# Layer 1's f and g on the two halves of TensorE's columns, with transfers to the quarters in place of copies

## The chip, the cores and the metric

The kernel runs on one core of one Trainium2 chip. The metric is the device time of that core in microseconds (us), the median of several executions. Below, TensorE is the matrix engine (PE in the profile, PEld for its weight loads), VectorE is DVE, ScalarE is ACT, GpSimd is POOL, and SyncE is SP, which issues all transfers (DMAs) of this kernel from one queue. Everything is in float32.

## What is computed

Eight images of 32x32 tokens (N = 1024) with C = 256 channels go through two attention layers. Layer 0 has four heads; layer 1 has one head whose f and g have only 32 channels.

```python
# layer 0: x (8, 32, 32, 256), W_qkv (256, 4*768), W_out (1024, 256)
xf = x.reshape(B, -1, C)
qkv = jnp.einsum('bnc,cd->bnd', xf, W_qkv).reshape(B, -1, h, 3 * C)
q, k, v = jnp.split(qkv, 3, axis=-1)
atten = jax.nn.softmax(jnp.einsum('bihd,bjhd->bijh', q, k) * scale, axis=2)
res = jnp.einsum('bijh,bjhd->bihd', atten, v).reshape(B, -1, h * C)
x = jnp.einsum('bnd,dc->bnc', res, W_out) + b_out + xf
# layer 1: Wf, Wg (256, 32), Wh (256, 256)
f = jnp.einsum('bhwc,ck->bhwk', x, Wf) + bf
g = jnp.einsum('bhwc,ck->bhwk', x, Wg) + bg
h = jnp.einsum('bhwc,cd->bhwd', x, Wh) + bh
s = jnp.einsum('bik,bjk->bij', g_flat, f_flat)
o = jnp.einsum('bij,bjd->bid', jax.nn.softmax(s, axis=-1), h_flat)
y = gamma * o + x
```

## The kernel before, in words

**Layer 0.** The weights of a head are folded first (`fold_weights`: query with key weights into wqk, value with output weights into wvo), so that a head needs one projection of x. The products of queries with keys, and of probabilities with values, are made by a scheme of seven products and sums of blocks (`seven`, line 235 for its matmuls, lines 252, 258 and 264 for what takes them out of the matmul banks). A head is worked off in two blocks of 512 query tokens.

**Layer 1.** The tokens after layer 0 are turned by transfers and VectorE (`turn_rows`) into x1T, channels on partitions. `Layer1.queries` projects x1T with `wfg_sb`, whose 128 columns hold Wf twice and Wg twice, 32 columns each: one matmul over 128 columns gives f on partitions 0 to 63 (twice) and g on partitions 64 to 127 (twice), for 512 tokens at a time (line 435, tile pm_fg). `store_fg` takes them out: ScalarE adds the bias on the 64 partitions where the result stands (line 661), and VectorE copies it to the other 64 partitions (line 662). In the end f and g stand four times each, on all four quarters of 32 partitions. `Layer1.scores` needs that: four matmuls with 32 rows of weights each, on the four quarters, make the scores of four times 128 keys (line 697, tile ps_l). `values` makes h (line 455), `Softmax` and `row_products` the rest (line 776).

**The order.** Each engine's order is the order in which the program issues its instructions. The main loop goes over `steps`: the heads of an image with two blocks each, and layer 1 of the image before put in after head 1 (after head 3 for the last but one image). Within a step, `put(tasks, *at)` gives each task a place on a scale from 0 to about 10, and the tasks are issued in order of place. In the step of head 1 (head 3), block 0, the turned tokens arrive; in the same head's block 1 the task list of `queries` stands at 1.4, 1.5 and 3.5: a start, the first 512 tokens, the second 512. The following step, block 0 of layer 1, begins with the scores. The last image has its own tail (`final`), which uses `queries` too.

Before the loop, x and the weights are loaded, the identity for transposes is built by VectorE, the first image is transposed by TensorE (line 339), and the weights of the four heads are folded, in part during the first step: `fold` is the list of the tasks for heads 1 to 3, five a head (three transposing, two multiplying, lines 291 and 307), and the first step places them among its scores.

**Buffers that matter here.** "m0" is one buffer, used by layer 0's sums of probabilities (`first` in `sums`, line 574, read again at line 579) and by layer 1's softmax. "psm" is a pair of matmul banks for everything but the scores and `seven`. "q" holds the queries of a head, or f and g of an image (`fg_tile`). "rs" is one small buffer for sums.

The functions that the diff touches:

Of the kernel before, what the change touches and what calls it, by code (L numbers as in the profile page):

```python
# [10 lines left out]
F32 = mybir.dt.float32  # L11
AF = mybir.ActivationFunctionType
# [4 lines left out]
P = 128  # L17
# [3 lines left out]
def kernel(  # L21
# [51 lines left out]
    nc = tc.nc  # L73
# [3 lines left out]
    CK = w_f.shape[1]  # L77
    CC = C // P
    NT = N // P
    NB = 512  # L80
    NBLK = N // NB
    HT = NB // P
# [10 lines left out]
    const = ctx.enter_context(tc.tile_pool(name="const", bufs=1))  # L93
# [15 lines left out]
    def tile_of(tag, shape, name):  # L109
        return pools[tag].tile(shape, F32, tag=tag, name=name)  # L110
# [4 lines left out]
    def load_x(b, parts=1):  # L115
        t = tile_of("rows", [P, NT, C], f"x_{b}")
        n = HT // parts
        for k in range(NBLK):
            for i in range(parts):
                nc.sync.dma_start(  # L120
                    t[:, k * HT + i * n : k * HT + (i + 1) * n, :].rearrange("p t c -> p (t c)"),
                    x_v[b][:, k, ts(i, n * C)],
                )
        rows[b] = t

    def identity():

        Q = 32
        t = const.tile([P, P], F32, tag="ident", name="ident")
        col = const.tile([P, Q], F32, tag="col", name="col")  # L130
        row = const.tile([P, Q], F32, tag="row", name="row")
        nc.vector.memset(col[:, 0:1], 0.0)
        w = 1
        while w < Q:
            nc.vector.tensor_scalar(col[:, w : 2 * w], col[:, :w], float(w), None, ALU.add)
            w *= 2
        nc.vector.transpose(row, col)
        nc.vector.memset(t, 0.0)
        for k in range(P // Q):
            r = ts(k, Q)  # L140
            nc.vector.tensor_tensor(t[r, r], col[r], row[r], ALU.is_equal)
        return t
# [4 lines left out]
    wfg_sb = const.tile([P, CC, P], F32, tag="wfg", name="wfg_sb")  # L147
    bout_sb = const.tile([P, C], F32, tag="bout", name="bout_sb")
    bfg_sb = const.tile([P, 1], F32, tag="bfg", name="bfg_sb")
    bh_sb = const.tile([P, C], F32, tag="bh", name="bh_sb")  # L150
    gamma_sb = const.tile([P, 1], F32, tag="gamma", name="gamma_sb")

# [2 lines left out]
    def load_rest():  # L155
        with nc.allow_non_contiguous_dma(reason="small bias vectors, loaded once"):
            nc.sync.dma_start(bout_sb, b_out.partition_broadcast(P))
            for r in range(P // CK):
                w, bias = (w_f, b_f) if r < P // CK // 2 else (w_g, b_g)
                nc.sync.dma_start(  # L160
                    wfg_sb[:, :, ts(r, CK)], w.rearrange("(cc p) k -> p cc k", p=P)
                )
                nc.sync.dma_start(bfg_sb[ts(r, CK), :], bias.unsqueeze(1))
            nc.sync.dma_start(wh_sb, w_h.rearrange("(cc p) d -> p cc d", p=P))
            nc.sync.dma_start(bh_sb, b_h.partition_broadcast(P))
            nc.sync.dma_start(gamma_sb, gamma.partition_broadcast(P))
# [12 lines left out]
    def load_weights(h, tag):  # L179

        nw = CC * 3 * C
        t = tile_of(tag, [P, nw + CC * C], f"w_{h}")
        w = t[:, :nw].rearrange("p (c d) -> p c d", c=CC)
        wo = t[:, nw:].rearrange("p (c d) -> p c d", c=CC)
        nc.sync.dma_start(w, wqkv_v[:, :, ts(h, 3 * C)])
        nc.sync.dma_start(wo, wout_v[:, ts(h, CC), :])
        weights[h] = w, wo
# [141 lines left out]
    xT_of, x1T_of, xblocks, vblocks = {}, {}, {}, {}  # L329
# [136 lines left out]
    def values_tile(name):  # L466
        v = tile_of("v", [P, NT, CV], name)
        nc.gpsimd.memset(v[:, :, C : C + 1], 1.0)
        return v
# [174 lines left out]
    class Layer1:  # L644
# [19 lines left out]
        def queries(self):  # L664
# [7 lines left out]
                f"fg_{b}", lambda: wfg_sb, P, lambda: x1T_of[b], self.store_fg  # L672
            )

        def values(self):
            def start():
                self.v = values_tile(f"v_{self.name}")

            return [start] + project_rows(
                f"v_{self.name}", lambda: wh_sb, lambda: x1T_of[self.b],  # L680
                lambda t2, pm: nc.vector.scalar_tensor_tensor(
                    self.v[:, 2 * t2 : 2 * t2 + 2, :C], pm, gamma_sb,
                    bh_sb.unsqueeze(1).broadcast_to([P, 2, C]), ALU.mult, ALU.add,
                ),
            )
# [127 lines left out]
        engines={mybir.EngineType.PE, mybir.EngineType.DVE, mybir.EngineType.Activation}  # L813
    ))
    load_x(0, 2)
    ident = identity()
    load_weights(0, "s")
    load_weights(1, "rows")
    load_weights(2, "v")
# [20 lines left out]
    fold = fold_weights(1) + fold_weights(2) + fold_weights(3)  # L840
# [6 lines left out]
    def step(k):  # L847
        return steps[k] if 0 <= k < len(steps) else None
# [4 lines left out]
    for i, (a, blk) in enumerate(steps):  # L853
        l0 = isinstance(a, Layer0)
        one, two, nxt = step(i - 1), step(i - 2), step(i + 1)
        places = []

        def put(tasks, *at):
            assert len(tasks) == len(at)
            places.extend(zip(at, range(len(places), len(places) + len(at)), tasks))  # L860

        if l0:
            put(a.scores(blk), 0, 2, 4, 6, 8, 10)
        else:
            tasks, pieces = a.scores(blk)
            put(tasks, *((0.5, 2.4) if blk == 0 else (0.5, 2)))
            put(pieces, *((1.6, 3.9, 6.2, 6.5, 7.4, 8.4, 8.6) if blk == 0 else
                          (0.9, 2.7, 4.2, 5, 6.2, 6.8, 7.5)))
        if is_l0(two):
            u, k = two  # L870
            put(u.products_of[k][2:], 1 if l0 else 0)
            put([partial(u.invert, k)], 2.9 if l0 or blk == 1 else 1.9)
            put(u.project(k), *((3, 7) if l0 else (2, 6) if blk == 0 else (3, 7)))
        if is_l0(one):
            u, k = one
            sums, keys = u.sums(k)
            u.products_of[k] = u.products(k)
            put(sums[:2] + sums[3:], *((2.2, 3.2, 4.2) if l0 else (0.8, 2.2, 4.5)))
            put(sums[2:3], 5.2 if l0 else 5.5)
            put(keys, *((6.2, 8.2) if l0 else (7.6, 9.6)))  # L880
            put(u.products_of[k][:2], *((5, 9) if l0 else (4, 7)))
        elif one is not None:
            put(one[0].products(one[1]), *((3, 5, 7, 9) if l0 else (1, 4, 6, 8)))
        if i == 0:
            put(fold[2:], -1, *[0.9 + 0.6 * n for n in range(len(fold) - 3)])
            put(first_sums[:2], 8.4, 9.4)
        if i == 1:
            put(first_sums[2:], 1.4, 3.4)
            put([partial(nc.vector.tensor_scalar, bh_sb, bh_sb, gamma_sb, None, ALU.mult)], 8.5)

        if is_l0(nxt) and blk == NBLK - 1:
            queries, qsums = nxt[0].queries()
            put(queries, *((2.5, 4.5, 6.5) if not l0 else
                            (1.5, 2.5, 4.5) if is_l0(two) else (0.5, 2.5, 5.5)))
            put(qsums, *((6.7, 6.9, 7.3, 7.6) if not l0 else
                          (5.4, 6.4, 7.2, 7.4) if is_l0(two) else (6.4, 7.2, 7.3, 7.4)))

        if l0 and a.h == 0 and blk == 0:
            put(residual(a.b), 5.3, 6.3, 7.3, 7.4)
        if l0 and a.h == 0 and blk == 1 and a.b > 0:  # L900
            put(value_sums(a.b), 1.4, 2.4, 3.4, 4.4)
        if l0 and a.h == 2 and blk == 0 and a.b + 1 < B:
            load_x(a.b + 1)
        if l0 and a.h == 2 and blk == 1 and a.b + 1 < B:
            moves, squares = turn_rows(a.b + 1, rows, xT_of, 0)
            put(moves, *range(1, 9))
        if l0 and a.h == HEADS - 1 and blk == 0 and a.b + 1 < B:
            put(squares, 0.4, 1.4, 2.4, 4.4)
            put(key_sums(a.b + 1), 5.4, 6.4, 7.2, 7.4)

        if l0 and a.b > 0 and a.h == behind(a.b) - 1:
            if blk == 0:
                moves, turned = turn_rows(a.b - 1, rows1, x1T_of, 1, step(i + 2)[0].fg_tile)
                put(moves, 0.1, 0.2, 0.3, 0.4)
                put(turned, 5.4, 6.4, 7.2, 7.4)
            else:
                put(nxt[0].queries(), 1.4, 1.5, 3.5)
        if not l0 and blk == 0:
            put(a.values(), 0.9, 1, 3, 5, 8)
        if nxt is None:  # L920
            put(transpose_rows(B - 1, rows1, x1T_of, 1), 8.1, 8.2, 8.3, 8.4)
            put(final.queries(), 9, 9.1, 9.3)
        for _, _, t in sorted(places, key=lambda x: x[:2]):
            t()
# [136 lines left out]
```

## Time and profile before

Three executions took 2358.72, 2360.36 and 2360.5 us; the profiled one took 2358.68 us, with a span of 2356.9 us in the profile and a mean granted TensorE clock of 0.999.

| group of instructions | what it is | count | busy us | mean ns |
|---|---|---|---|---|
| line 235, psy, TensorE | one of the score products of layer 0 | 1024 | 262.9 | 379 |
| line 626, po, TensorE | output projection of layer 0 | 1024 | 242.0 | 379 |
| line 776, pa_l, TensorE | layer 1, probabilities by values | 1024 | 231.7 | 381 |
| line 697, ps_l, TensorE | layer 1, scores on row quarters | 256 | 36.5 | 640 |
| line 366, fg<-x, SP | transfers that turn layer 1's tokens, 64 KB each | 112 | - | 2.3 us to landing |
| lines 586 and 589, SP | a row of sums turned into columns | 64 each | - | 2.1 us to landing (589) |

Busy time is what the records cover; matmul records overlap their neighbours, so the mean of one is longer than the time from one start to the next. In a group's line of the profile, what follows the second bar is the idle time of that engine just before these instructions, and what ended it.

### The profile page before, as it was taken

The numbers are of one execution on the slowest core, as the hardware profiler recorded it, in microseconds if no ns is written. First come the engines' busy times: TensorE is split into PE (matmuls) and PEld (weight loads), VectorE is DVE, ScalarE is ACT, GpSimd is POOL, SyncE is SP. The second block draws the span as 40 slices with busy tenths as digits, with TensorE's granted clock in tenths as the row PEclk, the third lists the DMA queues.
The fourth block names the chain that finished last, engine by engine and source line by source line (L and its number), as shares of the span: only waits on it lengthen the run. The fifth ranks groups of instructions, "written<-read, shape, count | busy, mean of one in ns | idle before, by whom it ended". The sixth has DMA issues, their size and how long they took to land.

```text
span 2356.9 us, 26075 instructions
## 1 busy us (share of the span) xinstructions
PE 2336.5 (99%) x10384; PEld 1923.2 (82%) x10384; DVE 1617.1 (69%) x2533; ACT 590.7 (25%) x945; POOL 236.6 (10%) x93
## 2 busy tenths in 40 slices
PE   8999999999999999999999999999999999999998
PEld 6888888788877888788887888878888788888877
DVE  5667777577775767767777577676776757766665
ACT  2222223222232222322223222232222322212232
POOL 0111110011110111101111011110001101100110
PEclk9999999999999999999999999999999999999999
DMA  4000010100101001010010000110001100000100
GB/s 136 1 1 1 1 36 4 34 1 9 28 5 32 1 19 19 8 29 1 19 19 13 24 1 19 19 17 20 1 19 19 19 18 1 1 1 1 19 10 29
DMA packets 163602, 38.35 MB, mean 16 GB/s; under 512 B 156112, under 2 KB 158160, under 8 KB 163472
## 3 DMA queue, kind: packets, MB, share of 16 engines
q1 hardware_dynamic: 163472, 36.60, 7.6%
q8 instruction: 84, 1.38, 0.2%
q14 instruction: 46, 0.38, 0.1%
HBM read 13.37 MB, written 8.52 MB: 9 GB/s over the span
## 4 chain that ended last, share of the span: by engine, by line
PE 95%; DVE 4%; DMA 0%; ACT 0%; issue 0%; SPq 0%; DVEq 0%; ACTq 0%
PE psy L235 14%; PE psy_y L235 14%; PE pa_l L776 9%; PE psx L235 9%; PE psz L235 9%; PE po L626 9%; PE psx_y L235 9%; PE psz_y L235 9%; PE psy_q L235 4%; PE psx_q L235 2%; PE psz_q L235 2%; PE pr_v_l L455 2%; PE pm_fg L435 1%; PE ps_l L697 1%; DVE s_l L758 1%; DVE s L569 0%
## 5 line engine op out<-in xcount | busy, mean ns | idle before, releaser
L582 POOL PARTITION_ALL_REDUCE rb<-rs x64 | 207.0, 3234 | 1891.5 <-DVE rs L580 1891.5
L530 ACT ACTIVATE p<-p 128x1024 f32<-128x1024 f32 x128 | 135.3, 1057 | 536.8 <-DVE p L252 536.8
L235 PE MATMUL psy<-qs,xs 128*128 128x256 f32 x1024 | 262.9, 379 | 1.7 <-DVE qs L501 1.7
L235 PE MATMUL psx<-q,x0T 128*128 128x256 f32 x1024 | 262.8, 379 | 0.0
L235 PE MATMUL psz<-q,xs 128*128 128x256 f32 x1024 | 262.8, 379 | 0.0
L235 PE MATMUL psy_y<-s,xt 128*128 128x256 f32 x1024 | 243.0, 380 | 2.5 <-DVE s L569 2.4
L626 PE MATMUL po<-wvo,y 128*128 128x256 f32 x1024 | 242.0, 379 | 0.0
L235 PE MATMUL psx_y<-p,x 128*128 128x256 f32 x1024 | 241.9, 379 | 0.0
L776 PE MATMUL pa_l<-v_l,s_l 128*128 128x257 f32 x1024 | 231.7, 381 | 2.3 <-DVE y L252 1.9
L235 PEld LDWEIGHTS psx<-q,x0T 128*128 128x128 f32 x1024 | 194.4, 190 | 43.0 <-issue 18.2
L626 PEld LDWEIGHTS po<-wvo,y 128*128 128x128 f32 x1024 | 194.5, 190 | 40.0 <-issue 15.1
L776 PEld LDWEIGHTS pa_l<-v_l,s_l 128*128 128x128 f32 x1024 | 193.7, 190 | 39.0 <-issue 12.6
L235 PEld LDWEIGHTS psx_y<-p,x 128*128 128x128 f32 x1024 | 194.6, 190 | 34.1 <-issue 8.6
L235 PEld LDWEIGHTS psy_y<-s,xt 128*128 128x128 f32 x1024 | 192.2, 190 | 34.7 <-PE psx_y L235 5.0
L235 PEld LDWEIGHTS psy<-qs,xs 128*128 128x128 f32 x1024 | 194.5, 190 | 28.5 <-DVE qs L501 2.1
L235 PEld LDWEIGHTS psz<-q,xs 128*128 128x128 f32 x1024 | 194.6, 190 | 26.5
L252 DVE TENSOR_TENSOR u<-psy,e 128x512 f32<-128x512 f32 x128 | 88.5, 691 | 148.1 <-PE psy L235 74.7
L264 ACT ACTIVATE p<-psx 128x512 f32<-128x512 f32 x128 | 76.4, 597 | 409.7 <-PE psx L235 409.5
L252 DVE TENSOR_TENSOR v<-psy,e 128x512 f32<-128x512 f32 x128 | 87.9, 687 | 101.8 <-PE psy L235 101.6
L235 PE MATMUL psy<-qs,x0T 128*128 128x256 f32 x512 | 131.5, 379 | 0.8 <-DVE v L252 0.8
L258 ACT COPY e<-psx 128x512 f32<-128x512 f32 x128 | 73.9, 577 | 202.3 <-PE psx L235 202.3
L637 DVE SCALAR_TENSOR_TENSOR x<-po,inverse,x 128x256 f32<-128x256 f32 x256 | 111.9, 478 | 17.6 <-PE po L626 7.3
(110 smaller groups left out, 3091.1 us busy)
## 6 DMA issues: line engine op xcount, KB each, us to landing
out_dram<-x SPq DMA_DIRECT2D x15, 512.0 KB, 2.6
x<-in_x_dram SPq DMA_DIRECT2D x14, 512.0 KB, 4.6
x0T<-x SPq DMA_DIRECT2D x224, 32.0 KB, 2.0
fg<-x SPq DMA_DIRECT2D x112, 64.0 KB, 2.3
w<-in_L_conv_W_qkv_dram SPq DMA_DIRECT2D x4, 768.0 KB
x<-in_x_dram SPq DMA_DIRECT2D x4, 256.0 KB, 4.5
w<-in_L_conv_W_out_dram SPq DMA_DIRECT2D x4, 256.0 KB, 9.5
line<-rb SPq DMA_DIRECT2D x64, 2.0 KB
```

The lines of the kernel that those rows point to most:

```text
L235: nc.tensor.matmul(banks[k][:, ts(i, w)], lhsT=lhsT, rhs=rhs, start=first and n == 0, stop=True, skip_group_check=True,)
L252: nc.vector.tensor_tensor(dst, shaped(banks[k]), shaped(other), ALU.add)
L258: nc.scalar.copy(scratch("e"), banks["x"])
L264: copy(outs["11"](), shaped(banks["x"]))
L435: nc.tensor.matmul(pm[:m], lhsT=w()[:, c, d * P : d * P + m], rhs=src()[:, c, ts(k, NB)], start=(c == 0), stop=(c == CC - 1),)
L455: nc.tensor.matmul(pm[:, ts(j, C)], lhsT=src()[:, c, ts(2 * t2 + j, P)], rhs=w()[:, c, :], start=(c == 0), stop=(c == CC - 1),)
L530: exp(both, both)
L582: nc.gpsimd.partition_all_reduce(t, r.rearrange("p e i -> p (e i)"), P, bass_isa.ReduceOp.add)
L626: nc.tensor.matmul(pm[:, ts(j, C)], lhsT=self.y[blk][:, c, ts(2 * t2 + j, P)], rhs=folded[self.h][1][:, c, :], start=(c == 0), stop=(c == ...
L637: nc.vector.scalar_tensor_tensor(acc, pm[:, ts(j, C)], inverse[:, n : n + 1], acc, ALU.mult, ALU.add)
L697: nc.tensor.matmul(pm, lhsT=self.f[ts(r, CK), ts(j0 + r, P)], rhs=self.g[ts(r, CK), ts(blk, NB)], start=True, stop=True,)
L776: nc.tensor.matmul(pm[:, : C + 1], lhsT=p[:, j, ts(ti, P)], rhs=v[:, j, : C + 1], start=(j == 0), stop=(j == NT - 1),)
```

## The change

There are three parts.

1. For images 0 to 6, `queries_apart` takes the place of `queries` in the loop. It uses only 64 of the columns of `wfg_sb`, those that hold Wf once and Wg once. The first 512 tokens go to columns 0 to 63 and so to partitions 0 to 63 of one bank, the second 512 tokens to columns 64 to 127 and partitions 64 to 127 of another bank; the four matmuls are issued in turn (first half, second half, then the same for the other 128 channels). Two activations on ScalarE add the bias (a second bias tile, `bfg2_sb`, has it in the order f, g, f, g) and put the result into a tile in the buffer m0. From there 16 transfers an image bring f and g to the four quarters, f only those 128-token pieces that a quarter's matmuls read, g whole. The copies on VectorE are gone. All matmuls stand at place 1.5, the transfers at 1.6 to 1.9.
2. Before the first transposes, VectorE clears a tile (`idle`) and TensorE multiplies it with itself five times; nothing reads the result.
3. In the first step, the task `multiply` wqk of head 1 moves from place 0.9 to ahead of the scores.

```diff
+    bfg2_sb = const.tile([P, 1], F32, tag="bfg2", name="bfg2_sb")
...
+                nc.sync.dma_start(bfg2_sb[ts(r, CK), :], (b_f, b_g)[r % 2].unsqueeze(1))
...
+        def queries_apart(self):
+            b = self.b
+            half, quarters = P // 2, P // CK
+            made = {}
+
+            def task():
+                fg = self.fg_tile()
+                self.f, self.g = fg[:, 0, :], fg[:, 1, :]
+                made["t"] = t = tile_of("m0", [P, NB], f"fg2_{b}")
+                w = wfg_sb[:, :, half - CK : half + CK]
+                pms = [tile_of("psm", [P, NB], f"pm_fg{k}_{b}") for k in range(NBLK)]
+                for c in range(CC):
+                    for k, pm in enumerate(pms):
+                        nc.tensor.matmul(
+                            pm[ts(k, half)],
+                            lhsT=w[:, c, :],
+                            rhs=x1T_of[b][:, c, ts(k, NB)],
+                            start=(c == 0),
+                            stop=(c == CC - 1),
+                        )
+                for k, pm in enumerate(pms):
+                    r = ts(k, half)
+                    nc.scalar.activation(t[r], pm[r], AF.Identity, bias=bfg2_sb[r])
+
+            def move(r):
+                q = ts(r, CK)
+                for k in range(NBLK):
+                    f, g = (made["t"][k * half + i * CK : k * half + (i + 1) * CK] for i in range(2))
+                    nc.sync.dma_start(self.f[q, ts(k * HT + r, P)], f[:, ts(r, P)])
+                    nc.sync.dma_start(self.g[q, ts(k, NB)], g)
+
+            return [task], [partial(move, r) for r in range(quarters)]
...
+    idle = tile_of("rs", [P, P], "idle")
+    nc.vector.memset(idle, 0.0)
     ident = identity()
+    pm = tile_of("psm", [P, NB], "pm_idle")
+    for _ in range(5):
+        nc.tensor.matmul(pm[:, :P], lhsT=idle, rhs=idle, start=True, stop=True)
...
         if i == 0:
-            put(fold[2:], -1, *[0.9 + 0.6 * n for n in range(len(fold) - 3)])
+            put(fold[2:], -2, -1, *[1.5 + 0.6 * n for n in range(len(fold) - 4)])
...
             else:
-                put(nxt[0].queries(), 1.4, 1.5, 3.5)
+                tasks, moves = nxt[0].queries_apart()
+                put(tasks, 1.5)
+                put(moves, 1.6, 1.7, 1.8, 1.9)
```

## The prediction

> **What bounds the kernel now.** I read the page from its first part down: busy time, the chain that ended last, the groups of the stage that changes; then the timeline of one image's stage, the DMA queue around it, and the start.
>
> ```profile
> PE 2336.5 (99%) x10384; PEld 1923.2 (82%) x10384; DVE 1617.1 (69%) x2533; ACT 590.7 (25%) x945; POOL 236.6 (10%) x93
> PE 95%; DVE 4%; DMA 0%; ACT 0%; issue 0%; SPq 0%; DVEq 0%; ACTq 0%
> L435 PE MATMUL pm_fg<-x1T,wfg_sb 128*128 128x512 f32 x64 | 30.0, 594 | 0.2 <-ACT x1T L342 0.2
> L661 ACT ACTIVATE fg<-pm_fg,bfg_sb 64x512 f32<-64x512 f32 x32 | 21.8, 683 | 65.4 <-PE pm_fg L435 65.0
> L662 DVE COPY fg<-fg 64x512 f32<-64x512 f32 x32 | 13.5, 422 | 22.1 <-ACT fg L661 21.7
> ```
>
> TensorE is idle for 20 of 2357 us and carries 95% of the chain: a stretch is worth what it takes or gives TensorE. The copies at L662 wait for L661, and hardly anything on TensorE waits for either. "x64" is 8 images by 4 matmuls by 2 records: an f32 matmul leaves two. Matmuls overlap, so I take the distance from start to start. The stage of image 0 in the timeline (start, duration, engine, operation):
>
> ```profile
> 358.19 1.88 PE L435 MATMUL pm_fg<-x1T,wfg_sb 128*128 128x512 f32 x4
> 359.91 1.03 PE L235 MATMUL psx<-q,x0T 128*128 128x256 f32 x4
> 363.36 1.88 PE L435 MATMUL pm_fg<-x1T,wfg_sb 128*128 128x512 f32 x4
> 365.08 1.03 PE L235 MATMUL psy<-qs,x0T 128*128 128x256 f32 x4
> 384.94 1.89 PE L235 MATMUL psz_y<-ss,x 128*128 128x256 f32 x8
> 386.76 1.14 PE L697 MATMUL ps_l<-fg 32*128 32x512 f32 x8
> 387.83 1.99 PE L455 MATMUL pr_v_l<-wh_sb,x1T 128*128 128x256 f32 x8
> 389.66 1.89 PE L626 MATMUL po<-wvo,y 128*128 128x256 f32 x8
> ```
>
> Four records of 512 columns take 359.91-358.19 = 1.72 us, 0.43 each; eight of 256 columns also take 1.72. So f and g of an image cost 2 x 1.72 = 3.44 us of TensorE. The lower half shows what parts of the array can do: the scores put four matmuls on four groups of 32 rows, and their eight records take 1.07 us to the next start, where one after the other they would take 3.44.
>
> **What the Trainium skill says.** "TensorEngine Tiling (Array Packing)", section Key Properties: tiles work independently, and a change of tiling mode drains TensorE. Both show above. "TensorE: Matmul & The Clock Gate", section Measured speedup vs the span model: three column tiles gave 2.38 times, four row tiles 3.07; the row group here gives 3.44/1.07 = 3.2, and no run here shows columns. Same page, Part 1: TensorE starts at half clock until about 3.4 us of activity. The first transposes do run slowly, but that is over when the weights land (below).
>
> **The change part by part.**
>
> *f and g on column halves, images 0 to 6.* Eight records of 64 columns of weights replace eight of 128; pairs that stand on different halves can run together, so four rounds of 0.43 = 1.72 us are the floor. To that comes the tiling. From the row group: the stage before it should give way at 384.94+1.72 = 386.66, the group starts 0.10 later; inside, two rounds take 1.07 for 0.86, 0.21 too many; the stage after it takes 1.83 for 1.72, 0.11 too many. Entry and exit are paid once (0.21); the 0.21 inside belongs to the group or to each two rounds. That bounds an image at 2.14 and 2.35; I take 2.25. Gain 3.44-2.25 = 1.19, times 7 = **8.3 us** (7.6 to 9.1). Row groups are not column groups, which no record shows: the ends beyond this are the rivals below.
>
> *Removed copies and half of the evictions.* 7x4 copies x 0.422 = 11.8 us of VectorE, 7x2 activations x 0.683 = 9.6 us of ScalarE. Price 0: both lie beside TensorE's 99%. They offset that TensorE comes earlier: v follows psy's start by 1.06 us (as at 378.23 below), so it would run at 362.36 instead of 361.99, and s, which TensorE's psy_y needs, would be done at 367.1, where TensorE arrives at 367.3. Bound 0.1 us an image.
>
> *Sixteen transfers an image (eight of 32x128, eight of 32x512), 112 in all, on SP's queue.* VectorE and SP in the same stretch:
>
> ```profile
> 354.45 0.38 SPq L589 DMA_DIRECT2D st<-line  x1
> 384.12 0.23 SPq L586 DMA_DIRECT2D line<-rb  x1
> 374.59 1.22 DVE L574 TENSOR_TENSOR m<-ss 128x1024 f32<-128x1024 f32 x1
> 376.51 0.88 DVE L637 SCALAR_TENSOR_TENSOR x<-po,inverse,x 128x256 f32<-128x256 f32 x2 [0.70 <-PE po L626]
> 378.23 0.69 DVE L252 TENSOR_TENSOR v<-psy,e 128x512 f32<-128x512 f32 x1 [0.85 <-PE psy L235]
> 381.48 1.03 PE L235 MATMUL psy<-qs,x0T 128*128 128x256 f32 x4
> 329.48 8.04 SPq L366 DMA_DIRECT2D fg<-x  x12
> ```
>
> ScalarE would finish at about 362. SP issued twelve fg<-x transfers in 8.04 us, 0.67 each, and those land after a median 2.3 us; so 16 x 0.67 = 10.7 and 2.3 later, by 375.0, all are there. The small st took SP 0.38, which would make it 370.4. SP is otherwise free from 355 to 384, so neither the line and st behind them nor POOL waits. TensorE's scores want f and g at about 385.5: hidden. The new wait is VectorE's m (L574): its buffer m0 is where the transfers read, so it now waits for all sixteen. Without one it would start at 374.59-1.19 = 373.4. Behind it in VectorE's order are x<-po and v, and TensorE's third psy (381.48, then 380.3) waits for v. From m to the end of v is 1.22+0.88+0.69 = 2.8, so m may start at 377.4 before TensorE loses anything. The landing at 370.4 to 375.0 costs 0 to 1.6 us of VectorE's idle time and nothing of TensorE's. Price 0. The semaphore waits in front of the scores lie on TensorE's queue and are satisfied by then; 0 (up to 0.1 an image). Both matmul buffers psm are taken at once; the next po needs one, freed by the first activation at 361.2, before po at 362.2; 0.
>
> *The start.* The multiply of weights 1 is moved ahead of the first scores:
>
> ```profile
> 21.75 1.03 PE L235 MATMUL psx<-q,x0T 128*128 128x256 f32 x4
> 24.51 1.13 PE L235 MATMUL psy<-qs,xs 128*128 128x256 f32 x4 [1.73 <-DVE qs L501]
> 26.34 1.89 PE L307 MATMUL pwqk<-wqT 128*128 128x256 f32 x8
> ```
>
> TensorE waits 1.73 us for VectorE's qs. pwqk (1.72) needs copies that end by 20.8 and now fits from 21.75 to 23.47; psx follows, psy keeps 24.51, and what came after pwqk comes 1.72 earlier. VectorE's u moves behind wqk and its sums, to 28.3; the second psy wants it at 28.8. **1.7 us** (0 to 1.8: a later wait could take it back, and nothing there makes it lose).
>
> *Zeros first.* Ten records and a memset of about 0.17 us while x is on its way; the first transpose waits for x until 4.0. The chain of waits goes through the arrival of the first weights at 8.76, and TensorE is at full clock from then on already (pwq's four records of 128 columns take 0.63 us, px's fourteen before took 3.34). 0 (to +1 in an execution where the clock rises later). Four more bias loads on SP delay wh, bh, gamma and the second x by some us; none is wanted before 60 us. 0.
>
> Sum: 8.3+1.7 = 10.0 us, against the profiled span of 2356.9: 2346.9. That execution took 2358.68 us; the others shown 2358.72 to 2360.5, median 2360.36. 2360.4-10.0 = **2350.4**.
>
> **The rivals.**
> 1. *Halves overlap only in part.* Each matmul's two records stand one after the other on the same half. If TensorE keeps that order, record 2 runs beside record 3 only, giving five rounds, 2.15+0.42 = 2.57: gain 0.87 x 7 + 1.7 = 7.8, at 2352.6. Against it: the row group, written in the same order, ran its four first records together.
> 2. *No overlap: the change doesn't do what it says.* Columns share the rows through which data and weights come; row groups do not, so their evidence need not carry over. Then 8 x 0.43 + 0.42 = 3.86, with 0.21 for each two rounds 4.5: 0.4 to 1.06 lost an image, 2.9 to 7.4 in all, less 1.7: 2361.6 to 2366.1.
> 3. *Slower: the wait at m0.* Place: VectorE's m at L574. If the sixteen land after 377.4, TensorE's psy waits as much longer; from 378.6 the gain on columns is gone, and from 379.5 (gain of the start used up, and 4.7 us more, over 7) the kernel is measurably slower. That needs 0.95 us a transfer. For it: while the weights load, SP's small wfg and bfg transfers come 2.73 us a pair, 1.37 each (issues at 11.48, 12.22, 14.21, 14.94, 16.94 and 17.68), since each waits for an earlier one. At 1.37, landing is at 362+21.9+2.3 = 386.2, 8.8 us late: 7 x (8.8-1.2)-1.7, so 2412. Against it: then the queues were full, here they are empty, and 0.67 was kept up through twelve transfers of more pieces.
>
> **How the numbers follow.** Full overlap 0.65 (gain 7.6 to 10.9: 2349.5 to 2352.8), part 0.13, none 0.13, m0 0.06, others 0.03. A measurement of this kernel can tell 0.2%, 4.7 us, from no change: the first two cases are faster than 2355.6; no overlap lies half within the bound and half above; m0 is slower. Faster 0.79, same 0.10, slower 0.11. The range: the bottom is an overlap without seams (7 x 1.72 + 1.8 = 13.8, 2346.6), the top takes in partial overlap with the gain of the start lost and some wait at m0: 2346.5 to 2358.5.
>
> **What would show it.** Right: 56 records of 64 columns whose image takes 2.1 to 2.4 us from first start to the next stage, in pairs some ns apart; psy at the start with no 1.7 us wait; m0's readers landed before 376. Wrong: the records 0.43 apart throughout (rival 2); a wait of VectorE at L574 for a DMA over 3 us, with a hole of TensorE before psy (rival 3); or a hole elsewhere in the stage as long as the gain.

## The result, and the profile after

The changed kernel takes 2347.29 us (median of 6 executions, 2346.37 to 2348.55), the kernel before, on the same chip, 2359.74 us (6 executions, 2357.71 to 2361.49): a ratio of 0.9948, with a 95% interval of 0.9935 to 0.9961. That is 12.4 us faster, in the range, and 3.1 us better than the 2350.4 forecast. The profiled execution took 2347.16 us with a span of 2345.4 us, against 2356.9 us before. In all comparisons of this document every execution lies within 0.2% of its kernel's median, but for one of the run e3 below, which took 6413.33 us and is not counted in its ratio.

The page of the kernel after, its busy times and its chain. Lines have moved: the scheme of seven products is at L237 now, the new matmuls are L693, their activations L702, the transfers L708 (f) and L709 (g), the last image's own L437, L663 and L664.

```profile
PE 2329.4 (99%) x10394; PEld 1917.0 (82%) x10394; DVE 1606.1 (68%) x2506; ACT 580.0 (25%) x931; POOL 236.5 (10%) x93
PE 95%; DVE 4%; DMA 0%; ACT 0%; issue 0%; SPq 0%; DVEq 0%; ACTq 0%
fg<-fg SPq DMA_DIRECT2D x56, 64.0 KB, 2.0
```

TensorE still carries 95% of the chain, so what is gained must be TensorE's. VectorE has 27 instructions fewer (28 copies removed, one memset added) and ScalarE 14. The groups of the stage:

```profile
L693 PE MATMUL pm_fg<-x1T,wfg_sb 128*64 128x512 f32 x56 | 13.6, 605 | 0.0
L702 ACT ACTIVATE fg<-pm_fg,bfg_sb 64x512 f32<-64x512 f32 x14 | 9.5, 682 | 42.1 <-PE pm_fg L693 42.0
L437 PE MATMUL pm_fg<-x1T,wfg_sb 128*128 128x512 f32 x8 | 3.7, 605 | 0.2 <-ACT x1T L344 0.2
L664 DVE COPY fg<-fg 64x512 f32<-64x512 f32 x4 | 1.7, 422 | 5.6 <-ACT fg L663 5.6
```

The records have a mean of 605 ns, about as long as before (594), but 56 of them cover 13.6 us, 1.94 an image, where 56 of the old ones stood 0.43 us apart and so took 24. The eight of the last image are of the old kind. The stage of image 0 in the timeline after (start, duration, engine, operation); the weight loads (PEld) show the order inside the group:

```profile
355.06 1.89 PE L237 MATMUL psz_y<-ss,x 128*128 128x256 f32 x8
356.88 0.20 PEld L693 LDWEIGHTS pm_fg<-x1T,wfg_sb 128*64 128x64 f32 x4 [0.33 <-issue]
356.88 1.94 PE L693 MATMUL pm_fg<-x1T,wfg_sb 128*64 128x512 f32 x8
357.36 0.14 PEld L693 LDWEIGHTS pm_fg<-x1T,wfg_sb 128*64 128x64 f32 x2 [0.29 <-issue]
357.79 0.14 PEld L693 LDWEIGHTS pm_fg<-x1T,wfg_sb 128*64 128x64 f32 x2 [0.29 <-issue]
358.75 1.13 PE L237 MATMUL psx<-q,x0T 128*128 128x256 f32 x4
```

Loads come in twos, 0.43 apart. Single records of the trace show the same of the matmuls: they start at 0 and 7 ns, 480 and 487, 910 and 916, 1339 and 1345 (image 3), and psx 1.87 us after the first. The two records that signal a finished half to ScalarE are both in the last pair, so a pair has one record of each half.

What the group costs beyond its four rounds of 0.43, I call its seams. psz_y should give way at 355.06+1.72 = 356.78, so the entry costs 0.10. Inside, the first round takes 0.48, 0.05 too many, and psx starts 0.53 after the last pair, 0.10 too many. At the exit, psx takes 0.10 more than its undisturbed 0.86. An image costs 1.87+0.20 = 2.07 us, that is 1.72 and 0.35 of seams, the same in all seven.

The transfers and what could wait for them, same timeline:

```profile
358.85 1.39 ACT L702 ACTIVATE fg<-pm_fg,bfg_sb 64x512 f32<-64x512 f32 x2 [6.00 <-PE pm_fg L693]
359.56 0.57 SPq L708 DMA_DIRECT2D fg<-fg  x1
...
369.54 0.59 SPq L709 DMA_DIRECT2D fg<-fg  x1
...
371.21 0.69 DVE L254 TENSOR_TENSOR u<-psy,e 128x512 f32<-128x512 f32 x1 [1.62 <-PE psy L237]
371.95 1.23 DVE L576 TENSOR_TENSOR m<-ss 128x1024 f32<-128x1024 f32 x1
373.73 0.88 DVE L639 SCALAR_TENSOR_TENSOR x<-po,inverse,x 128x256 f32<-128x256 f32 x2 [0.56 <-PE po L628]
375.45 0.69 DVE L254 TENSOR_TENSOR v<-psy,e 128x512 f32<-128x512 f32 x1 [0.85 <-PE psy L237]
378.71 1.03 PE L237 MATMUL psy<-qs,x0T 128*128 128x256 f32 x4
383.98 1.14 PE L735 MATMUL ps_l<-fg 32*128 32x512 f32 x8
```

The sixteenth transfer is issued at 369.54 and, by the median of 2.0, lands near 371.6. VectorE's m follows u at once, with no wait in brackets; psy and the scores have none either. (Over the seven images m waits for these transfers for 0.2 us at most, in image 6, and no wait of TensorE follows.) The start, where the fold moved:

```profile
9.20 0.63 PE L293 MATMUL pwq<-ident,w 128*128 128x128 f32 x4 [1.07 <-DMA w<-in_L_conv_W_qkv_dram]
...
22.06 1.89 PE L309 MATMUL pwqk<-wqT 128*128 128x256 f32 x8
23.79 1.03 PE L237 MATMUL psx<-q,x0T 128*128 128x256 f32 x4
24.82 1.13 PE L237 MATMUL psy<-qs,xs 128*128 128x256 f32 x4
```

The wait of 1.73 us in front of psy is gone; pwqk fills it. The weights landed 0.3 us later than in the profiled execution before (pwq at 9.20, then 8.90).

Where the time went: I compared the start of each TensorE record with its counterpart before. They are 0.31 later at 9 us, 1.41 earlier once the fold is done (so 1.72 gained), and then 2.78, 4.14, 5.49, 6.85, 8.20, 9.57 and 10.92 earlier after images 0 to 6. Nothing else on TensorE steps: seven times 1.36, and one 1.72. That makes 11.2 us. (The two profiled spans differ by 11.5: 0.3 was lost as the weights landed later, and 0.6 lies behind TensorE's last record: 6.1 us before, 5.4 to 5.9 in all the other traces.) The fastest executions of the two kernels lie 2357.71-2346.37 = 11.3 apart, so the remaining 1.2 of the 12.4 between the medians is in how the executions scatter.

### The profile page after: what moved, and what is told of

It is laid out like the page before. It is cut to its first block, busy times and chain, and to the rows that moved or that the text cites. A ratio compares the mean times of both kernels' runs of the same rounds, so it can differ in the third digit from the quotient of the medians.

```text
span 2345.4 us, 26265 instructions
## 1 busy us (share of the span) xinstructions
PE 2329.4 (99%) x10394; PEld 1917.0 (82%) x10394; DVE 1606.1 (68%) x2506; ACT 580.0 (25%) x931; POOL 236.5 (10%) x93
## 4 chain that ended last, share of the span: by engine, by line
PE 95%; DVE 4%; DMA 0%; ACT 0%; issue 0%; SPq 0%; DVEq 0%; ACTq 0%
PE psy L237 14%; PE psy_y L237 14%; PE psx L237 9%; PE pa_l L814 9%; PE psz L237 9%; PE po L628 9%; PE psx_y L237 9%; PE psz_y L237 9%; PE psy_q L237 4%; PE psx_q L237 2%; PE psz_q L237 2%; PE pr_v_l L457 2%; PE ps_l L735 1%; DVE s_l L796 1%; PE pm_fg L693 1%; DVE s L571 0%
## 5 line engine op out<-in xcount | busy, mean ns | idle before, releaser
L237 PE MATMUL psx<-q,x0T 128*128 128x256 f32 x1024 | 263.5, 380 | 0.0
L237 PE MATMUL psy<-qs,xs 128*128 128x256 f32 x1024 | 262.9, 379 | 0.0
L237 PE MATMUL psz<-q,xs 128*128 128x256 f32 x1024 | 262.8, 379 | 0.0
L237 PE MATMUL psy_y<-s,xt 128*128 128x256 f32 x1024 | 243.0, 380 | 2.6 <-DVE s L571 2.4
L237 PE MATMUL psx_y<-p,x 128*128 128x256 f32 x1024 | 241.9, 379 | 0.0
L237 PEld LDWEIGHTS psx<-q,x0T 128*128 128x128 f32 x1024 | 193.9, 190 | 45.4 <-issue 20.7
L628 PEld LDWEIGHTS po<-wvo,y 128*128 128x128 f32 x1024 | 194.5, 190 | 40.0 <-issue 15.1
L237 PEld LDWEIGHTS psx_y<-p,x 128*128 128x128 f32 x1024 | 194.6, 190 | 34.1 <-issue 8.6
L237 PEld LDWEIGHTS psy_y<-s,xt 128*128 128x128 f32 x1024 | 191.6, 190 | 35.4 <-PE psx_y L237 5.0
L237 PEld LDWEIGHTS psy<-qs,xs 128*128 128x128 f32 x1024 | 194.5, 190 | 26.8 <-DVE qs L503 0.4
L237 PEld LDWEIGHTS psz<-q,xs 128*128 128x128 f32 x1024 | 194.6, 190 | 26.4
L237 PE MATMUL psy<-qs,x0T 128*128 128x256 f32 x512 | 131.5, 379 | 0.8 <-DVE v L254 0.8
```

Source lines behind the costliest of these rows:

```text
L237: nc.tensor.matmul(banks[k][:, ts(i, w)], lhsT=lhsT, rhs=rhs, start=first and n == 0, stop=True, skip_group_check=True,)
L628: nc.tensor.matmul(pm[:, ts(j, C)], lhsT=self.y[blk][:, c, ts(2 * t2 + j, P)], rhs=folded[self.h][1][:, c, :], start=(c == 0), stop=(c == ...
```

## The experiments

Ratios are to the kernel before, run beside on the same chip.

**Each part alone.** Three kernels each have one part of the change and nothing else of it (e1 to e3), and a fourth leaves one part out (e4).

```diff
 e1_columns_only: the changed kernel without its zeros, and with the fold's old places
-    idle = tile_of("rs", [P, P], "idle")
-    nc.vector.memset(idle, 0.0)
-    pm = tile_of("psm", [P, NB], "pm_idle")
-    for _ in range(5):
-        nc.tensor.matmul(pm[:, :P], lhsT=idle, rhs=idle, start=True, stop=True)
-            put(fold[2:], -2, -1, *[1.5 + 0.6 * n for n in range(len(fold) - 4)])
+            put(fold[2:], -1, *[0.9 + 0.6 * n for n in range(len(fold) - 3)])
 e2_fold_only: the kernel before, with the fold's new places
-            put(fold[2:], -1, *[0.9 + 0.6 * n for n in range(len(fold) - 3)])
+            put(fold[2:], -2, -1, *[1.5 + 0.6 * n for n in range(len(fold) - 4)])
```

> The kernel before with the column halves and the transfers alone; no zeros, the folding in its old order. Theory: an image gains what its matmul group loses on TensorE, 3.43 - 2.07 = 1.37 us, seven times, so 9.6 us and nothing else: ratio 0.9959, about 2350. Rival: part of the gain of 12.4 us in the medians is a side effect of the other two parts, or the removed VectorE copies count as well (11.8 us of busy time): then this gives clearly less than 9 or more than 11 us.

Measured: 2350.38 us, 0.9955 (0.9942 to 0.9969). The group costs 2.07 us as in the whole change, and TensorE gains 1.36 with each image; the timeline still has the wait of 1.73 us in front of psy:

```profile
25.00 1.13 PE L237 MATMUL psy<-qs,xs 128*128 128x256 f32 x4 [1.73 <-DVE qs L503]
```

> The kernel before with only the multiply of weights 1 moved ahead of the first scores. Theory: it fills TensorE's wait of 1.73 us for qs and gains 1.7 us, ratio 0.9993; all later starts on TensorE move by 1.72 us. Rival: a later wait takes it back, ratio 1.000.

Measured: 2357.44 us, 0.999 (0.9983 to 0.9997). The wait in front of psy is gone here too, since pwqk runs before psx:

```profile
23.92 1.89 PE L307 MATMUL pwqk<-wqT 128*128 128x256 f32 x8
25.65 1.03 PE L235 MATMUL psx<-q,x0T 128*128 128x256 f32 x4
26.68 1.13 PE L235 MATMUL psy<-qs,xs 128*128 128x256 f32 x4
```

The medians give 9.7 and 2.7 us, which add up to the whole, though the intervals of the ratios leave each of them wide (7.3 to 13.7, and 0.7 to 4.0). Record by record the traces give 9.5 and 1.7, as in the whole change: the parts don't touch each other. The fold's median gains 1.0 more than its trace, inside its interval and about as much as the whole change gains over its own; where that comes from is not shown.

The zeros, added to the kernel before (e3) and left out of the changed one (e4):

```diff
 e3_zeros_only: the kernel before
+    idle = tile_of("rs", [P, P], "idle")
+    nc.vector.memset(idle, 0.0)
     ident = identity()
+    pm = tile_of("psm", [P, NB], "pm_idle")
+    for _ in range(5):
+        nc.tensor.matmul(pm[:, :P], lhsT=idle, rhs=idle, start=True, stop=True)
 e4_no_zeros: the changed kernel, with these five lines left out
```

> The kernel before with only the five multiplications of zeros at the start. Theory: nothing on the path, since the first weights land at 8.8 us and TensorE's clock is up by then: ratio 1.0000, px records at half speed as before. Rival: the zeros bring the clock up earlier, in the profile (px records of 128 columns at 0.11 instead of 0.21 us apart) or in those executions where it comes late: up to 1 us, ratio 0.9996, and a smaller scatter.

Measured: 2360.49 us, 1.0001 (0.9992 to 1.001).

> The changed kernel without the zeros: columns and folding. Theory: the parts add up, 9.6 + 1.7 = 11.3 us, ratio 0.9952. Rival: the zeros carry the rest of the measured 12.4 us, so about 1 us slower than the whole change (ratio 0.9948).

Measured: 2347.1 us, 0.9947 (0.9934 to 0.9961), against 0.9948 with them. The zeros are worth nothing that these runs can tell. The traces say why. With the zeros, in e3 and in the changed kernel, the transposes of x stand 0.21 us apart (0.11 is the distance at full clock), just as in the kernel before; x comes in pieces and leaves gaps between them. And after the transposes TensorE waits for the first weights anyway. From e3:

```profile
4.96 3.33 PE L339 MATMUL px<-ident,x 128*128 128x128 f32 x14 [0.42 <-DMA x<-in_x_dram]
9.32 0.63 PE L291 MATMUL pwq<-ident,w 128*128 128x128 f32 x4 [1.03 <-DMA w<-in_L_conv_W_qkv_dram]
```

**Do the halves run together by their order or by their columns?** First the loops are exchanged, so that a half's two matmuls, four records, are issued before the other half's.

```diff
 e5_half_after_half: the changed kernel
-                for c in range(CC):
-                    for k, pm in enumerate(pms):
+                for k, pm in enumerate(pms):
+                    for c in range(CC):
```

> The changed kernel with its two loops exchanged: all matmuls of the first half of the tokens, then all of the second. Nothing else changes. Theory A: TensorE takes records of different column halves out of order[...]; the first record of the second half now stands fifth instead of third, still near, so pairs start together, 2.07 us an image, and the time stays at 2347. Theory B: only near neighbours overlap; then at most one pair, some 3.2 us or, with none, 3.65 us an image: 8 to 11 us slower, 2355 to 2358.

Measured: 2347.12 us, 0.9945 (0.9928 to 0.9962). The weight loads of image 0 in its timeline:

```profile
360.37 0.20 PEld L693 LDWEIGHTS pm_fg<-x1T,wfg_sb 128*64 128x64 f32 x4 [0.33 <-issue]
360.85 0.15 PEld L693 LDWEIGHTS pm_fg<-x1T,wfg_sb 128*64 128x64 f32 x2 [0.28 <-issue]
361.28 0.15 PEld L693 LDWEIGHTS pm_fg<-x1T,wfg_sb 128*64 128x64 f32 x2 [0.28 <-issue]
362.24 0.73 PEld L237 LDWEIGHTS psx<-q,x0T 128*128 128x128 f32 x4 [0.81 <-issue]
```

Twos again, 0.43 apart, and 1.87 us to psx: the starts in a pair lie 13 ns apart instead of 7, and nothing else changes. A record of the second half has run beside the first of the first half, past three that were issued before it. The record that signals the first half's end was issued fourth, and it runs in the last pair (1.34 or 1.35 us after the start), beside the one that signals the second half's.

Then both halves go to the same 64 columns, in the two banks as before:

```diff
 e6_one_half: the changed kernel
-                            pm[ts(k, half)],
+                            pm[:half],
...
-                    nc.scalar.activation(t[r], pm[r], AF.Identity, bias=bfg2_sb[r])
+                    nc.scalar.activation(t[r], pm[:half], AF.Identity, bias=bfg2_sb[:half])
```

> The changed kernel with both halves of the tokens on columns 0 to 63, in two banks; the second activation moves its result from partitions 0 to 63 to 64 to 127. Same records, same order, same transfers. Theory: the gain is the overlap of the two column halves; without it eight records stand 0.43 apart, 3.43 and 0.2 to 0.3 for entry and exit, so 1.6 us an image lost, 11 us: 2358. Rival: 64 columns of weights or the new order are worth something by themselves: under 2354.

Measured: 2361.05 us, 1.0005 (0.9996 to 1.0014). Its weight loads:

```profile
358.89 0.19 PEld L693 LDWEIGHTS pm_fg<-x1T,wfg_sb 128*64 128x64 f32 x2 [0.33 <-issue]
359.38 0.14 PEld L693 LDWEIGHTS pm_fg<-x1T,wfg_sb 128*64 128x64 f32 x1 [0.29 <-issue]
359.81 0.14 PEld L693 LDWEIGHTS pm_fg<-x1T,wfg_sb 128*64 128x64 f32 x1 [0.29 <-issue]
...
362.47 0.73 PEld L237 LDWEIGHTS psx<-q,x0T 128*128 128x128 f32 x4 [0.81 <-ACT fg L702]
```

Single loads, 0.43 apart, and 3.58 us to psx: with entry and exit 3.78 an image, 1.71 more than the changed kernel, 12.0 us over seven. That is eight rounds, 3.43, and the same seams, 0.35. The mechanism came as expected, the size not quite: I had 3.6 to 3.7 an image and 2358. In the profiled execution TensorE loses 2.0 us more at the start, where it reached full clock only at 13.6 us. The copies and half of the evictions are gone in this kernel too, and it gains nothing by that.

**How near is the wait at m0?** Each transfer is cut into two, so that 32 an image are issued; the same bytes move.

```diff
 e7_transfers_doubled: the changed kernel
-                    nc.sync.dma_start(self.f[q, ts(k * HT + r, P)], f[:, ts(r, P)])
-                    nc.sync.dma_start(self.g[q, ts(k, NB)], g)
+                    for i in range(2):
+                        fi, gi = ts(2 * (k * HT + r) + i, P // 2), ts(2 * k + i, NB // 2)
+                        nc.sync.dma_start(self.f[q, fi], f[:, ts(2 * r + i, P // 2)])
+                        nc.sync.dma_start(self.g[q, gi], g[:, ts(i, NB // 2)])
```

> The changed kernel with each transfer cut in two (32 an image, same bytes). Theory: SP issues one in 0.63 us whatever its size, so the last lands at 359.6 + 20.2 + 2.0 = 381.7 in image 0. VectorE's sum into m0, due at 372.0, waits for it; TensorE stands it until 375.8 and then waits for v: 5.9 us an image, 41 us, about 2388. Rival: SP's queue does not matter because small transfers are issued faster, or VectorE's wait is hidden: 2347 to 2350.

Measured: 2406.86 us, 1.0204 (1.0187 to 1.0221). The last issue, and the engines behind it, in the timeline of image 0:

```profile
383.46 0.59 SPq L711 DMA_DIRECT2D fg<-fg  x1
...
385.72 1.23 DVE L576 TENSOR_TENSOR m<-ss 128x1024 f32<-128x1024 f32 x1 [10.41 <-DMA fg<-fg]
...
387.65 0.68 DVE L254 TENSOR_TENSOR v<-psy,e 128x512 f32<-128x512 f32 x1
...
388.39 2.08 PE L237 MATMUL psy<-qs,x0T 128*128 128x256 f32 x4 [6.11 <-DVE v L254]
...
390.25 1.72 PE L237 MATMUL psz<-q,xs 128*128 128x256 f32 x4
...
391.81 1.89 PE L237 MATMUL psy_y<-p,xt 128*128 128x256 f32 x8
```

VectorE's m waits 10.41 us for the transfers, and TensorE's psy 6.11 for v. So far it is as predicted: I had a hole of 5.9. What I had not is in the next lines: from psy to psz it is 1.86 us and from psz to psy_y 1.56, where both took 0.86 or 0.87 in the changed kernel. The windows of the same trace (the stretch, its length, the busy times of PE, PEld, DVE, ACT and POOL with their instructions, the granted clock of TensorE, the DMA share, GB/s):

```profile
345.00:385.00 40.00, 37.28 (x172) 30.99 (x170) 19.68 (x31) 8.38 (x14) 3.24 (x1) 1.00 0.08 17
385.00:392.00 7.00, 3.61 (x9) 2.96 (x10) 5.68 (x10) 0.46 (x1) 1.73 (x1) 0.53 0.00 0
392.00:420.00 28.00, 28.00 (x135) 22.88 (x134) 22.30 (x28) 9.04 (x15) 3.29 (x2) 1.00 0.03 4
```

After the hole TensorE runs at half clock (0.53 over the 7 us) until about 392. Record by record against the changed kernel, image 0 loses 6.27 us to the hole and 1.69 to the clock. Over the seven images the holes come to 40.2 us, where 41 were expected, and the clock to 15.4 (1.5 to 3.0 an image); 3.4 more are lost at the start of this execution. The expected 2388 lacked the clock and the start.

The same kernel, with the tile in another buffer (rb, which GpSimd's all-reduce over partitions writes next):

```diff
 e8_doubled_other_buffer: e7 and
-                made["t"] = t = tile_of("m0", [P, NB], f"fg2_{b}")
+                made["t"] = t = tile_of("rb", [P, NB], f"fg2_{b}")
```

> As the run with doubled transfers, but the tile that they read stands in the buffer of GpSimd's all-reduce (rb) instead of m0. Theory: the loss comes through the buffer m0 and VectorE's wait alone. GpSimd now waits instead, due at 378.1, until 381.7; the line of sums comes 3.6 us later, which its reader at 388.9 stands: 2347 to 2350, though SP's queue is just as long. Rival: the long queue itself does the harm, through line and st behind it or through f and g arriving late at the scores: some 20 us or more slower here too.

Measured: 2348.96 us, 0.9955 (0.9939 to 0.9972), with a span of 2345.1 us in the profiled execution, as short as that of the changed kernel. From its timeline:

```profile
371.69 1.21 DVE L576 TENSOR_TENSOR m<-ss 128x1024 f32<-128x1024 f32 x1
...
378.58 1.03 PE L237 MATMUL psy<-qs,x0T 128*128 128x256 f32 x4
379.17 0.59 SPq L710 DMA_DIRECT2D fg<-fg  x1
379.80 0.59 SPq L711 DMA_DIRECT2D fg<-fg  x1
```

m and psy run without a wait, while transfers are still being issued. GpSimd starts its all-reduce at 382.22 instead of 378.09 us, which holds up nothing on TensorE. So what e7 loses in this stage goes through the buffer m0; sixteen more issues on SP cost TensorE nothing by themselves.

**Can zeros help at all?** They are made more and spread, so that TensorE has something to do in the gaps between pieces of x.

```diff
 e9_zeros_fill: the changed kernel
-    pm = tile_of("psm", [P, NB], "pm_idle")
-    for _ in range(5):
-        nc.tensor.matmul(pm[:, :P], lhsT=idle, rhs=idle, start=True, stop=True)
+    pm = tile_of("ps", [P, NB], "pm_idle")
+    def zeros(n):
+        for _ in range(n):
+            nc.tensor.matmul(pm[:, :P], lhsT=idle, rhs=idle, start=True, stop=True)
+    zeros(7)
...
-    run(transpose_rows(0, rows, xT_of, 0), [turn_q, turn_k, sums[0], turn_v], sums[1:3])
+    for t in transpose_rows(0, rows, xT_of, 0):
+        t()
+        zeros(1)
+    zeros(1)
+    run([turn_q, turn_k, sums[0], turn_v], sums[1:3])
```

> The changed kernel with more zeros and placed otherwise: in a bank of the scores, seven multiplies ahead of the first transposes, one more after each transpose of x and one ahead of the first weights' transpose, so that TensorE has work in the gaps of 0.2 us and more between the transposes. Theory A (the five zeros of the change did nothing because x leaves gaps behind them; without gaps the full clock comes before the weights do, in every execution): the late transposes of x stand 0.11 apart instead of 0.21, full clock before 8.5 us, the spread between executions shrinks and the median gains 0 to 1.5 us: ratio to the kernel before 0.9942 to 0.9948. Theory B (the start waits for the first weights, at 8.8 to 9.2 us, whatever the clock): the clock may rise earlier, the ratio stays at 0.9948 and the stages after the weights start as before. If the ten more multiplies stand ahead of the weights' transposes and delay them, the ratio is up to 0.0004 higher.

Measured: 2347.3 us (2347.04 to 2347.52, 5 executions), 0.9947 (0.9934 to 0.9961). Its start:

```profile
1.05 3.35 PE L861 MATMUL pm_idle<-idle 128*128 128x128 f32 x14 [1.05 <-DVE col L132]
4.20 0.63 PE L341 MATMUL px<-ident,x 128*128 128x128 f32 x2
...
7.71 0.60 PE L341 MATMUL px<-ident,x 128*128 128x128 f32 x4
8.14 0.61 PE L861 MATMUL pm_idle<-idle 128*128 128x128 f32 x4
9.30 0.63 PE L293 MATMUL pwq<-ident,w 128*128 128x128 f32 x4 [0.55 <-DMA w<-in_L_conv_W_qkv_dram]
```

Theory A holds for the clock: the records are 0.11 apart from 5.9 us on (four px in 0.60), 2.8 us before the changed kernel has its full clock (8.75). Theory B holds for the time: pwq waits for the weights and starts at 9.30, no earlier. The median does not move, so no version beats the changed kernel here. The five executions lie within 0.5 us, where those of the changed kernel spread over 2.2 and others of these kernels over up to 4.5; that the zeros cut off executions with a late clock is likely, but five executions don't prove it.

## Why the prediction was right, and where its sizes were off

*f and g on column halves* (taken at 2.25 us an image, bounds 2.14 and 2.35, gain 8.3): the mechanism was right, one term of the sum was mis-sized. An image measured 2.07, below its own lower bound; the gain is 1.36 an image, 9.5 us. The floor of 1.72 held, and so did entry and exit (0.10 each; 0.10 and 0.11 forecast). The mis-sized term is the seam inside the group, from its first start to that of psx. It was taken over from the row group as 0.21, once or for each two rounds (0.32 in the middle), and it measured 1.87-1.72 = 0.15, once: 0.05 in the first round, 0.10 after the last, and nothing in the rounds between. Single records of the row group before show where its 0.21 lay: its second round starts 0.53 after the first, and the next stage 0.54 after the second. Both of its two rounds were thus some 0.10 too long, which left open whether rounds between a first and a last pay as well. With columns they don't, and the first round is cheaper (0.05). Two halves give 3.44/1.87 = 1.84 times. The Trainium skill's "TensorE: Matmul & The Clock Gate", Measured speedup vs the span model, has 2.38 times for three column tiles; the two here come nearer to their number.

*The start* (1.7): 1.72, and nothing took it back.

*Zeros* (0): 0, by e3, e4 and e9, for the reason given: the weights' arrival bounds that stretch. "TensorE: Matmul & The Clock Gate", Part 1, of the Trainium skill, puts the start's half clock at about 3.4 us of activity. Here, with gaps in the activity, full clock came later than that in every trace: 3.7 us (e4) to 15.1 us (e5) after TensorE's first record. On the clock of the span it came between 7.6 and 16.1 us in the profiled executions but two, latest where a pause fell among the transposes (starts 1.49 us apart in e6, 1.66 in e2, 2.06 in e5). The two are e9, whose denser zeros had it at 5.9, and e7, which had it at 5.9, lost it at 9.4 and had it again at 16.2.

*Removed copies and evictions* (0), *psm* (0): TensorE waits 0.2 us for a copy once in the whole kernel, for the last image, before and after alike. psy_y starts at 365.76, as soon as psx_y gives way, though that was only 0.2 us from a wait in the forecast.

*Sixteen transfers* (0): SP took 0.63 from one to the next, where 0.67 was taken, and once 1.14; by the median they land at about 371.6, in the forecast 370.4 to 375.0. The tolerance was less than I said, since TensorE is earlier than reckoned: psy at 378.71 less 2.8 leaves m until 375.9 (377.4 forecast), 4.3 us after landing. At 0.63 each that is, by estimate, room for six more transfers an image, and not for sixteen, as e7 shows.

*The sum* (10.0): 9.5+1.7 = 11.2 along TensorE. The other 1.2 of the 12.4 between the medians is no step of TensorE in any trace; the kernel's own executions spread over 2.2 us and the interval of the ratio is 3 us to each side, so it is left as scatter.

*Rival 1* (five rounds) failed in its premise that TensorE keeps the order of issue. Each pair holds one record of each half: the two records that signal a half's end share the last pair, and e6 shows that records of one half stand 0.43 apart. In order, the second record of the first half would have come between. *Rival 2* (no overlap) is the case of e6, and it lands at 2361.05, 0.5 us under the 2361.6 to 2366.1 worked out: had columns not worked side by side, the change would have lost what the fold gains. *Rival 3* (the wait at m0) is real in all its steps, as e7 shows line by line, and at 1.37 us a transfer it would have been worse than worked out, if holes of 8.8 us cost clock as those of e7 (5.1 to 6.3 us) do. It was kept out by the 0.63 us of an issue; the 1.37 that spoke for it was measured while the weights load.

## What to carry to other kernels

A matmul that needs only half of TensorE's columns can share its time with another one. Here two of equal length, on different halves and in two banks (one bank was not tried), took the time of one and 0.35 us a group: 0.10 at the entry, 0.05 in the first round, 0.10 after the last and 0.10 at the exit, in either of two orders of issue. Pay for the spread of the result with transfers only after finding who next writes the buffer that they read, and how long that writer may wait; and count issues, not bytes (64 KB and 8 KB took SP the same 0.63 us here). Price a hole in the bounding engine above its length where its clock falls behind it: in e7 by 1.5 to 3.0 us for a hole of 5.1 to 6.3.

## What the runs showed that I had not expected

- Of eight records on two halves of columns, TensorE runs the pairs that can run together even when three others are issued between them (e5: 13 ns apart instead of 7). How it picks them is not shown.
- In the hole of 6.1 us in image 0 of e7 the granted clock of TensorE falls to half at 384.8, and comes back only at 391.6, 3.2 us after work has begun again: 1.7 us lost on top of the hole. Half clock lasts 6.83 us there, at the start and in four other images, and 3.41 in the remaining two.
- SP takes 0.63 us from one transfer to the next for 64 and 16 KB (g and f of the changed kernel) and for 32 and 8 KB (e7) alike: a transfer cut in two costs twice the issue time.
- When TensorE first reaches full clock differs by 10 us between the profiled executions (5.9 to 16.1 us); e7 had it early, fell back to half from 9.4 to 16.2, and lost 3.4 us at the start.
